# Adjacency, row and biases written into PSUM banks ahead of TensorE, in a four-layer graph kernel

## The chip, the cores and the metric

The kernel runs on one core of a Trainium2 chip. The metric is the device time of that core in microseconds. Before the change it is 4798.81 us, the median of three runs (4797.05 to 4799.08).

## The reference

Sixty-four graphs of 256 nodes with 128 features go through four layers, float32 throughout. All share one weighted adjacency matrix `adj` (256 x 256). Each layer is pre-normalised and residual: `h = relu(layernorm(x))`, `x = x + layer(h)`.

- Layer 0 is a gated recurrent graph network of five steps: a node mix `adj @ h`, two sigmoid gates, a tanh candidate, `h = (1 - z) h + z hv`.
- Layer 1 mixes `h` with Chebyshev powers of `adj`, multiplies by weights, adds `bias1` and takes the ReLU.
- Layer 2 computes `(adj @ h + h) @ weight + bias2` and divides each row by its norm.
- Layer 3 is an attention over all pairs of nodes:

```python
pre = s1[:, :, None, :] + s2[:, None, :, :] + b_lin     # 256 x 256 pairs x 256 features
h = jnp.where(pre >= 0, pre, ALPHA * pre)
e = jnp.einsum('bije,e->bij', h, a) + bias              # bias is adj
attn = jax.nn.softmax(e, axis=2)
out = jax.nn.sigmoid(jnp.einsum('bij,bjf->bif', attn, x))
```

Layer 3 is most of the work: for each graph 65,536 pairs of nodes times 256 features, a nonlinearity, and a sum over features.

## The kernel before, in words

Graphs are worked on two at a time: 32 pairs of graphs. For each pair a *front* computes layers 0 to 2 and the operands of layer 3. The first pair's two graphs have a front each (called alone). Then come the scores. A *unit* is half a pair's scores: 128 nodes of each of the two graphs against all 256 nodes, so there are 64 units, and each has one PSUM bank of 128 x 512 values that gathers its scores. A unit has 32 rows of slots with two halves of the features each, 64 half-slots. A *tile* is 128 features x 4 rows x 2 x 256 nodes (128 x 2048 values): a minimum or a ReLU of one operand against a per-partition scalar. Three engines make tiles in parallel: VectorE in one instruction (L928, one operand in PSUM, one in SBUF), ScalarE in eight (L940), GpSimd in eight (L945). For 600 slots the two halves are added by a DMA that GpSimd issues (L965). TensorE then multiplies each tile by a window of the weight vector and accumulates the result into the unit's bank (L1004).

When a unit's bank is complete, its *tail* (`tail`, L803) adds the *linear row*, a part of the score that depends only on the second node (`lin`, a half of the tile `rows`, spread to all partitions by DMA): L809. It then adds the last feature (L814), takes the maximum, the exponential, the product with the nodes' values, and writes the output.

The adjacency comes into the bank first of all: at a unit's first tile, `score` (L989) takes a bank and lets TensorE multiply the identity by `adj_n` (L998, in the helper L403), with the flag that starts an accumulation. `side_by_side` (L400) makes each 128-wide product of four 32-wide matmuls.

In the front, layer 1's products go into a bank by `project_token`, and VectorE adds `bias1` in place (L664) before it forms `x2`. Layer 2 does the same with `bias2` (L687), after which ScalarE squares it.

There are eight banks. One holds an operand of ScalarE's tiles for the whole run, one an operand of VectorE's tiles for as long as a pair needs it, at most two belong to units (`banks_of`), and the rest goes round among fronts and tails.

The order of instructions on each engine is fixed when the program is built, by a planner. It keeps a clock for each engine. `ran` (L107) adds the assumed duration of a piece of work, and returns when others may count on its result: the end, a constant for each engine, and for ScalarE a lag (`behind`) that grows by 2.4% of its work and shrinks while it has nothing to do. Fronts and tails are generators that yield the engine of their next step and the time from which it may run. The main loop takes the engine whose clock is earliest and gives it the first ready thing by rank: tails, fronts, scores or row additions, tiles. Engines run their queues in this order and wait for each other by semaphores.

Of the kernel before, what the change touches and what calls it, by code (L numbers as in the profile page):

```python
# [32 lines left out]
def kernel(  # L33
# [87 lines left out]
    def take():  # L121

        spare.sort(key=lambda b: b[1])
        return spare.pop(0)
# [280 lines left out]
    def flat(t):  # L405
        return t.rearrange("p b n -> p (b n)")

    def project(pp, w, t, start=True, stop=True):

        side_by_side(pp[:, 0:t.shape[1] * N], w, flat(t), start, stop)  # L410

    def mix_nodes(pm, h, a):

        nb = h.shape[1]
        pm = by_feature(pm, nb)
# [20 lines left out]
    def project_token(pp, pairs):  # L436

        nb = pairs[0][0].shape[1]
        pp = by_token(pp, nb)
# [45 lines left out]
    def front(p, batches):  # L485
# [165 lines left out]
        hT, t = copied("hT", b, t, bufs=4)  # L651
        yield PE, t_h, 1
# [5 lines left out]
        yield PE, t, 1  # L658
        po = take()
        project_token(po[0], [(hT, th[:, 0, :]), (c1T, th[:, 1, :]), (c2T, th[:, 2, :])])  # L660
        t = ran(PE, PRODUCTS[nb], t, po[1])
        yield DVE, t
        pt = rows_of(turned_of(po))
        nc.vector.tensor_add(pt, pt, bias1.unsqueeze(1).to_broadcast([P, nb * NC, D]))  # L664
        t = ran(DVE, ELEMENTS[nb], t)
        yield DVE, t
# [7 lines left out]
        t = yield from norm(x2, t, h)  # L674
        yield PE, t, 1
# [5 lines left out]
        yield PE, t, 1  # L681
        po = take()
        project_token(po[0], [(yT, w2)])
        t = ran(PE, PRODUCT[nb], t, po[1])
        yield DVE, t
        pt = rows_of(turned_of(po))
        nc.vector.tensor_add(pt, pt, bias2.unsqueeze(1).to_broadcast([P, nb * NC, D]))  # L687
        t = ran(DVE, ELEMENTS[nb], t)
# [114 lines left out]
    def tail(u, pe, since):  # L803

        ops = READY[u]
        x3, h3, pe, lin = ops["x3"], ops["h3"], [by_feature(pe[0])[:, k, :] for k in range(NB)], ops["lin"]
        yield DVE, max(since, ops["t_lin"])
        used = banks_of.pop(u)
        nc.vector.tensor_add(by_feature(used), by_feature(used), lin.to_broadcast([P, NB, N]) if ops["alone"] else lin)  # L809
        t = ran(DVE, ELEMENTS[2], since, ops["t_lin"])  # L810
        yield DVE, t
# [3 lines left out]
        t = ran(DVE, 0.8, t)  # L815
# [156 lines left out]

    def score_ready():

        best = None
        for tile_ in made:
            u, _ = where(tile_[1])
            since = tile_[0]
            if u not in left:
                if len(banks_of) == 2 or not spare:  # L980
                    continue
                since = max(since, min(b[1] for b in spare))
            if best is None or since < best[0]:
                best = since, tile_
        return best
# [3 lines left out]
    def score(tile_):  # L989
        since, n, k, t, e = tile_  # L990
        u, r = where(n)
        made.remove(tile_)
        if u not in left:
            left[u] = 64
            bank, free = take()
            banks_of[u] = bank
            for x, (_, c) in enumerate(across(u)):
                side_by_side(by_feature(bank)[:, x, :], ident, adj_n[:, c, :], x == 0, False)  # L998
            ran(PE, 0.87, since, free)
        left[u] -= 2 if k == 2 else 1  # L1000
        pe = banks_of[u]
        w = win if e == ACT else win_n
        for g in range(4):
            nc.tensor.matmul(pe[g * 32:(g + 1) * 32, :], w[:, 31 - r:63 - r], flat(t[:, g]),  # L1004
                             start=False, stop=(left[u] == 0), skip_group_check=True)
# [26 lines left out]
    def chain_ready(key, e):  # L1032

        engine, since, bank, gate = (*CHAINS[key][1], 0, None)[:4] if len(CHAINS[key][1]) < 4 else CHAINS[key][1]
        if engine != e or bank and not spare or gate and not gate():
            return None
# [5 lines left out]
        return max(since, min(b[1] for b in spare)) if bank else since  # L1042
# [15 lines left out]
    while scored[0] < 2 * NSLOT or CHAINS:  # L1058
# [20 lines left out]
        if ready:  # L1079
# [5 lines left out]
            elif e == PE:  # L1085
                score(what)
            elif rank == 2:
# [39 lines left out]
```

## Time and profile before

| | |
|---|---|
| median of 3 runs | 4798.81 us |
| the profiled execution, its own time | 4796.37 us |
| its span | 4794.6 us |
| TensorE matmul busy | 4744.3 us (99%) |
| VectorE busy | 4651.6 us (97%) |
| ScalarE busy | 4608.6 us (96%) |
| GpSimd busy | 4636.5 us (97%) |
| granted TensorE clock, mean | 0.999 |

The engines are PE (TensorE's matmuls), PEld (its weight loads), DVE (VectorE), ACT (ScalarE), POOL (GpSimd) and SP (SyncE). L928 means line 928 of the kernel before. A group's line has the engine, the operation, what is written from what, the shapes and the count, then the busy time, the mean of one, and the idle time in front of it with what ended it. Busy time counts what is in flight: an instruction that overlaps the one before it looks longer than the step from start to start. The ends of matmuls are modelled.

### The profile page before, as it was taken

The page shows a single profiled execution, that of the slowest core. Times are in us where ns is not written, and L with a number is a line of the kernel's source. Part 1 is how long each engine was busy: PE and PEld are TensorE (multiplying, and loading weights), DVE is VectorE, ACT ScalarE, POOL GpSimd, SP SyncE. Part 2 cuts the span into 40 slices and gives each one's busy share as a digit, 9 for nine tenths or more (in the row PEclk, how much of TensorE's full clock was granted, in tenths as well). Part 3 has the DMA queues.
Part 4 walks back from the last instruction along what each step waited for, and adds up shares of the span by engine and source line. Part 5 has one row for each costly group of instructions (what it writes and reads, how often), then busy time and mean ns, then how long its engine had stood idle before and what let it go on. Part 6 is the DMA issues. An engine that isn't in the chain of part 4 may idle for free.

```text
span 4794.6 us, 134766 instructions
## 1 busy us (share of the span) xinstructions
PE 4744.3 (99%) x52583; PEld 1758.2 (37%) x52583; DVE 4651.6 (97%) x3568; ACT 4608.6 (96%) x12063; POOL 4636.5 (97%) x9919
## 2 busy tenths in 40 slices
PE   9999999999999999999999999999999999999999
PEld 4333333433333333333333333333333333333333
DVE  6999999999999999999999999999999999999999
ACT  6999999999999999999999999999999999999999
POOL 3999999999999999999999999999999999999998
PEclk9999999999999999999999999999999999999999
DMA  1767777777676777777777777777767777777730
GB/s 39 151 142 154 150 146 150 145 145 158 141 157 143 143 155 152 151 146 145 149 152 149 147 150 146 151 155 146 148 138 158 150 151 151 148 150 143 151 66 5
DMA packets 131529, 672.82 MB, mean 140 GB/s; under 512 B 14920, under 2 KB 50120, under 8 KB 54088
## 3 DMA queue, kind: packets, MB, share of 16 engines
q0 software_dynamic: 86400, 629.18, 65.6%
q1 hardware_dynamic: 43768, 35.01, 2.5%
q8 instruction: 411, 6.73, 0.6%
q14 instruction: 230, 1.88, 0.1%
q10 hardware_dynamic: 720, 0.00, 0.0%
HBM read 26.48 MB, written 8.52 MB: 7 GB/s over the span
## 4 chain that ended last, share of the span: by engine, by line
PE 69%; DVE 10%; POOL 8%; DMA 6%; ACT 5%; issue 2%; POOLq 0%; SPq 0%; DVEq 0%; ACTq 0%
PE bank L1004 43%; PE bank L403 23%; DVE rl L928 8%; POOL rl L945 7%; DMA rl<-rl 5%; ACT rl L940 3%; PE bank L434 2%; PE bank L426 1%; POOL rl L965 1%; ACT h L478 0%; DVE bank L613 0%; DVE d L609 0%; DVE hT L617 0%; DVE rh L574 0%; POOL mv L398 0%
## 5 line engine op out<-in xcount | busy, mean ns | idle before, releaser
L940 ACT ACTIVATE rl<-bank,s1b 128x256 f32<-128x256 f32 x9976 | 3937.4, 704 | 47.5 <-DMA rl<-rl 18.7
L928 DVE TENSOR_TENSOR rl<-s1a,bank 128x2048 f32<-128x2048 f32 x1747 | 3909.3, 2276 | 41.4 <-DMA rl<-rl 19.5
L945 POOL TENSOR_SCALAR rl<-s2n,s1b 128x256 f32<-128x256 f32 x6408 | 3056.0, 799 | 19.5 <-ACT s1b L780 5.1
L1004 PE MATMUL bank<-rl,win_n 128*32 128x512 f32 x17992 | 2241.6, 593 | 20.8 <-DMA rl<-rl 14.9
L1004 PE MATMUL bank<-rl,win 128*32 128x512 f32 x9976 | 1317.3, 593 | 0.0
L945 POOL TENSOR_SCALAR rl<-s2c,s1a 128x256 f32<-128x256 f32 x2408 | 1167.1, 763 | 3.5
L1004 PEld LDWEIGHTS bank<-rl,win_n 128*32 128x32 f32 x17992 | 577.4, 110 | 1197.8 <-issue 978.2
L965 POOL DMA_DIRECT2D rl<-rl x600 | 644.9, 1090 | 3.6 <-PE bank L1004 0.9
L1004 PEld LDWEIGHTS bank<-rl,win 128*32 128x32 f32 x9976 | 324.8, 110 | 636.4 <-issue 516.5
L403 PE MATMUL bank<-mT,wts 128*32 128x512 f32 x2480 | 328.1, 592 | 0.5 <-ACT mT L526 0.5
L403 PE MATMUL bank<-adj_t,h 128*32 128x256 f32 x4960 | 296.8, 379 | 3.8 <-ACT h L628 3.8
L403 PEld LDWEIGHTS bank<-adj_t,h 128*32 128x32 f32 x4960 | 160.0, 110 | 160.8 <-issue 49.6
L478 ACT ACTIVATE h<-x,mv 128x128 f32<-128x128 f32 x376 | 163.8, 584 | 26.8 <-POOL mv L474 26.5
L403 PE MATMUL bank<-mT,w 128*32 128x512 f32 x1240 | 165.3, 593 | 0.6 <-ACT bank L570 0.5
L570 ACT ACTIVATE bank<-bank,gate_b 128x512 f32<-128x512 f32 (+1 forms) x165 | 137.6, 834 | 29.4 <-PE bank L403 16.5
L403 PE MATMUL bank<-rh,u5t 128*32 128x512 f32 x1240 | 164.9, 592 | 0.0
L403 PE MATMUL bank<-hT,wts 128*32 128x512 f32 x1240 | 163.5, 593 | 0.0
L403 PEld LDWEIGHTS bank<-mT,wts 128*32 128x32 f32 x2480 | 82.3, 110 | 185.1 <-issue 149.4
L398 POOL TENSOR_TENSOR mv<-mv,minus_half 128x4 f32<-128x4 f32 (+1 forms) x132 | 133.8, 1014 | 11.0
L593 ACT ACTIVATE bank<-bank,gate_b 128x512 f32<-128x512 f32 (+1 forms) x165 | 134.6, 816 | 10.2 <-PE bank L403 10.1
L526 ACT COPY mT<-bank 128x512 f32<-128x512 f32 x155 | 123.8, 799 | 19.6 <-PE bank L403 19.6
L606 ACT ACTIVATE bank<-bank,gate_b 128x512 f32<-128x512 f32 x155 | 128.8, 831 | 6.3 <-PE bank L403 6.3
(206 smaller groups left out, 3274.2 us busy)
## 6 DMA issues: line engine op xcount, KB each, us to landing
rl<-rl POOLq DMA_DIRECT2D x600, 1024.0 KB, 8.3
rows<-row SPq DMA_DIRECT2D x31, 512.0 KB
xin<-in_x_dram SPq DMA_DIRECT2D x64, 128.0 KB
out_dram<-o SPq DMA_DIRECT2D x64, 128.0 KB
row<-quarter SPq DMA_DIRECT2D x62, 2.0 KB
rows<-row SPq DMA_DIRECT2D x2, 256.0 KB
w_raw<-in_L_gnn_w_w_dram SPq DMA_DIRECT2D x3, 128.0 KB
rl<-in_L_gnn_Theta_dram SPq DMA_DIRECT2D x1, 320.0 KB
```

What stands on the lines that cost most here:

```text
L398: nc.gpsimd.tensor_tensor(t, t, minus_half[:, 0:t.shape[1]], op=OP.pow)
L403: nc.tensor.matmul(o[g:g + 32], w[:, g:g + 32], t, start=start, stop=stop, skip_group_check=True)
L478: nc.scalar.activation(h[:, k, :], s[:, k, :], AF.Relu, bias=mv[:, k, 0:1], scale=mv[:, k, 1:2])
L526: nc.scalar.copy(c, seen(bank))
L570: nc.scalar.activation(seen(r), seen(pr), AF.Tanh, bias=br, scale=0.5)
L593: nc.scalar.activation(seen(pr), seen(pr), AF.Tanh, bias=bz, scale=0.5)
L606: nc.scalar.activation(seen(pv), seen(pv), AF.Tanh, bias=bh_n, scale=-1.0)
L928: nc.vector.tensor_tensor(t, rows.to_broadcast(whole), ops["s2a"].unsqueeze(1).to_broadcast(whole), op=OP.min)
L940: nc.scalar.activation(t[:, g, b, :], other(ops["s2p"][0], b), AF.Relu, bias=rows[:, g, b], scale=-1.0)
L945: nc.gpsimd.tensor_scalar(t[:, part, b, :], other(ops["s2n" if k else "s2c"], b), rows[:, part, b], MOST_NEGATIVE, op0=OP.min, op1=OP.max)
L965: nc.gpsimd.dma_start(out=t.rearrange("p g b n -> p (g b n)"), in_=z.rearrange("p g b n -> p (g b n)"), accum_op=OP.add)
L1004: nc.tensor.matmul(pe[g * 32:(g + 1) * 32, :], w[:, 31 - r:63 - r], flat(t[:, g]), start=False, stop=(left[u] == 0), skip_group_check=True)
```

## The change

Three things change.

- **Adjacency and row.** For all units but the first pair's two, TensorE's product of identity and `adj_n` goes away. Instead VectorE writes `adj_n + lin` into the unit's bank before its first tile is scored (`fill_bank`, when `bank_ready` allows it). TensorE accumulates onto it from the first tile. The addition of the row in the tail goes away.
- **Biases.** For all fronts but the first pair's, ScalarE copies `bias1` or `bias2` into the bank that the products will use, and TensorE accumulates onto it. VectorE's two additions go away. The bank is taken before the last node mix instead of after it.
- **The planner.** ScalarE's lag goes away. Banks that a matmul has filled completely are kept in a set, `WRITTEN`, and only those are used for banks that another engine writes first. In the node mix and the token product only the first matmul of the whole bank carries the starting flag.

```diff
 SEEN = {PE: 0.25, DVE: 0.14, ACT: 0.18, POOL: 0.13}
-    behind = [0.0]
 
     def ran(engine, us, *after):
         start = max(clock[engine], 0.0, *after)
-        if engine == ACT:
-            behind[0] = max(0.0, behind[0] - (start - clock[ACT])) + 0.024 * us
         clock[engine] = start + us
-        return clock[engine] + SEEN[engine] + (behind[0] if engine == ACT else 0.0)
+        return clock[engine] + SEEN[engine]
...
-    def take():
-
-        spare.sort(key=lambda b: b[1])
-        return spare.pop(0)
+    WRITTEN = set()
+
+    def of_spare(bank):
+
+        return [b for b in spare if bank < 2 or id(b[0]) in WRITTEN]
+
+    def take(bank=1):
+
+        b = min(of_spare(bank), key=lambda b: (max(b[1], min(now.values())), bank < 2 and id(b[0]) in WRITTEN, b[1]))
+        spare.remove(b)
+        if bank < 2:
+            WRITTEN.discard(id(b[0]))
+        return b
+
+    def written(bank, nb):
+
+        if nb == NB:
+            WRITTEN.add(id(bank))
...
-                side_by_side(pm[:, b, :], h[:, b, c, :], a[:, c, :], c == 0, c == NC - 1)
+                side_by_side(pm[:, b, :], h[:, b, c, :], a[:, c, :], b == c == 0, c == NC - 1)
...
-                    side_by_side(pp[:, b, c, :], t[:, b, c * P:(c + 1) * P], w, k == 0, k == len(pairs) - 1)
+                    side_by_side(pp[:, b, c, :], t[:, b, c * P:(c + 1) * P], w, fresh and b == c == k == 0, k == len(pairs) - 1)
...
         hT, t = copied("hT", b, t, bufs=4)
+        if not alone:
+            yield ACT, t, 2
+            po = take(2)
+            nc.scalar.copy(rows_of(turned_of(po)), bias1.unsqueeze(1).to_broadcast([P, nb * NC, D]))
+            t_po = ran(ACT, COPY[nb], po[1])
         yield PE, t_h, 1
         b = take()
         mix_nodes(b[0], h, adj_2)
...
         yield DVE, t
-        pt = rows_of(turned_of(po))
-        nc.vector.tensor_add(pt, pt, bias1.unsqueeze(1).to_broadcast([P, nb * NC, D]))
-        t = ran(DVE, ELEMENTS[nb], t)
-        yield DVE, t
+        if alone:
+            pt = rows_of(turned_of(po))
+            nc.vector.tensor_add(pt, pt, bias1.unsqueeze(1).to_broadcast([P, nb * NC, D]))
+            t = ran(DVE, ELEMENTS[nb], t)
+            yield DVE, t
...
         yield DVE, max(since, ops["t_lin"])
-        used = banks_of.pop(u)
-        nc.vector.tensor_add(by_feature(used), by_feature(used), lin.to_broadcast([P, NB, N]) if ops["alone"] else lin)
-        t = ran(DVE, ELEMENTS[2], since, ops["t_lin"])
-        yield DVE, t
+        used = banks_of.pop(u)[0]
+        if ops["alone"]:
+            nc.vector.tensor_add(by_feature(used), by_feature(used), ops["lin"].to_broadcast([P, NB, N]))
+            since = ran(DVE, ELEMENTS[2], since, ops["t_lin"])
+            yield DVE, since
...
+    UNITS = [where(n)[0] for n in range(0, NSLOT, SLOTS // 2)]
+
+    def bank_ready():
+
+        u = next((u for u in UNITS if u not in left and u not in banks_of), None)
+        if u not in READY or READY[u]["alone"] or len(banks_of) == 2 or all(where(slot(k))[0] < u for k in range(3)):
+            return None
+        return (max(READY[u]["t_lin"], min(b[1] for b in of_spare(2))), u) if of_spare(2) else None
+
+    def fill_bank(u):
+        bank, free = take(2)
+        nc.vector.tensor_add(by_feature(bank), adj_n[:, u[1]:u[1] + 1, :].to_broadcast([P, NB, N]), READY[u]["lin"])
+        banks_of[u] = bank, ran(DVE, ELEMENTS[2], free, READY[u]["t_lin"])
...
-        if u not in left:
-            left[u] = 64
+        if u not in banks_of:
             bank, free = take()
-            banks_of[u] = bank
+            banks_of[u] = bank, free
             for x, (_, c) in enumerate(across(u)):
                 side_by_side(by_feature(bank)[:, x, :], ident, adj_n[:, c, :], x == 0, False)
             ran(PE, 0.87, since, free)
+            written(bank, NB)
+        left.setdefault(u, 64)
...
+            if e == DVE and bank_ready():
+                todo.append((bank_ready()[0], (2,), bank_ready()[1]))
```

More of the change, by code (lines that the diff above doesn't have):

```diff
@@ L410, in project @@
         side_by_side(pp[:, 0:t.shape[1] * N], w, flat(t), start, stop)
+        written(pp, t.shape[1])
     def mix_nodes(pm, h, a):
         nb = h.shape[1]
+        written(pm, nb)
         pm = by_feature(pm, nb)
@@ L434, in to_token, with project_token @@
                 nc.tensor.transpose(pt[:, b, c, :], ht[:, b, c * P:(c + 1) * P], ident)
-    def project_token(pp, pairs):
+    def project_token(pp, pairs, fresh=True):
         nb = pairs[0][0].shape[1]
+        written(pp, nb)
         pp = by_token(pp, nb)
@@ L657, in front @@
         c2T, t = copied("c2T", b, t)
[L658 to L661, printed above, removed]
-        yield DVE, t
-        pt = rows_of(turned_of(po))
-        nc.vector.tensor_add(pt, pt, bias1.unsqueeze(1).to_broadcast([P, nb * NC, D]))
-        t = ran(DVE, ELEMENTS[nb], t)
-        yield DVE, t
+        yield PE, t if alone else max(t, t_po), alone
+        if alone:
+            po = take()
+            t_po = po[1]
+        project_token(po[0], [(hT, th[:, 0, :]), (c1T, th[:, 1, :]), (c2T, th[:, 2, :])], fresh=alone)
+        t = ran(PE, PRODUCTS[nb], t, t_po)
+        yield DVE, t
+        if alone:
+            pt = rows_of(turned_of(po))
+            nc.vector.tensor_add(pt, pt, bias1.unsqueeze(1).to_broadcast([P, nb * NC, D]))
+            t = ran(DVE, ELEMENTS[nb], t)
+            yield DVE, t
         x2 = token("x2", tag="x12", bufs=3)
@@ L674, in front @@
         t = yield from norm(x2, t, h)
+        if not alone:
+            yield ACT, t, 2
+            po = take(2)
+            pt = rows_of(turned_of(po))
+            nc.scalar.copy(pt, bias2.unsqueeze(1).to_broadcast([P, nb * NC, D]))
+            t_po = ran(ACT, COPY[nb], po[1])
         yield PE, t, 1
@@ L680, in front @@
         yT, t = copied("yT", b, t)
[L681 to L684, printed above, removed]
-        yield DVE, t
-        pt = rows_of(turned_of(po))
-        nc.vector.tensor_add(pt, pt, bias2.unsqueeze(1).to_broadcast([P, nb * NC, D]))
-        t = ran(DVE, ELEMENTS[nb], t)
+        yield PE, t if alone else max(t, t_po), alone
+        if alone:
+            po = take()
+            t_po = po[1]
+        project_token(po[0], [(yT, w2)], fresh=alone)
+        t = ran(PE, PRODUCT[nb], t, t_po)
+        if alone:
+            yield DVE, t
+            pt = rows_of(turned_of(po))
+            nc.vector.tensor_add(pt, pt, bias2.unsqueeze(1).to_broadcast([P, nb * NC, D]))
+            t = ran(DVE, ELEMENTS[nb], t)
         yield ACT, t
@@ L805, in tail @@
         ops = READY[u]
-        x3, h3, pe, lin = ops["x3"], ops["h3"], [by_feature(pe[0])[:, k, :] for k in range(NB)], ops["lin"]
+        x3, h3, pe = ops["x3"], ops["h3"], [by_feature(pe[0])[:, k, :] for k in range(NB)]
         yield DVE, max(since, ops["t_lin"])
-        used = banks_of.pop(u)
-        nc.vector.tensor_add(by_feature(used), by_feature(used), lin.to_broadcast([P, NB, N]) if ops["alone"] else lin)
-        t = ran(DVE, ELEMENTS[2], since, ops["t_lin"])
-        yield DVE, t
+        used = banks_of.pop(u)[0]
[3 more added lines that the diff above has]
+            yield DVE, since
         sc = feat("sc", **SHORT)
@@ L814, in tail @@
             nc.vector.scalar_tensor_tensor(sc[:, k, :], ops["s2o"][:, b, :], ops["s1o"][:, b, c:c + 1], pe[k], op0=OP.min, op1=OP.add)
-        t = ran(DVE, 0.8, t)
+        t = ran(DVE, 0.8, since)
         spare.append([used, t])
@@ L979, in score_ready @@
             if u not in left:
-                if len(banks_of) == 2 or not spare:
+                if not READY[u]["alone"] and u not in banks_of or READY[u]["alone"] and (len(banks_of) == 2 or not spare):
                     continue
-                since = max(since, min(b[1] for b in spare))
+                since = max(since, banks_of[u][1] if u in banks_of else min(b[1] for b in spare))
             if best is None or since < best[0]:
@@ L999, in score @@
             ran(PE, 0.87, since, free)
+            written(bank, NB)
+        left.setdefault(u, 64)
         left[u] -= 2 if k == 2 else 1
-        pe = banks_of[u]
+        pe = banks_of[u][0]
         w = win if e == ACT else win_n
@@ L1034, in chain_ready @@
         engine, since, bank, gate = (*CHAINS[key][1], 0, None)[:4] if len(CHAINS[key][1]) < 4 else CHAINS[key][1]
-        if engine != e or bank and not spare or gate and not gate():
+        free = of_spare(bank)
+        if engine != e or bank and not free or gate and not gate():
             return None
@@ L1041, in chain_ready @@
                 return None
-        return max(since, min(b[1] for b in spare)) if bank else since
+        return max(since, min(b[1] for b in free)) if bank else since
     def advance(key):
@@ L1086 @@
                 score(what)
+            elif e == DVE and rank == 2:
+                fill_bank(what)
             elif rank == 2:
```

## The prediction

> **What bounds the kernel now.** I read the page's first part, then busy time by stretch, then the waits of single engines, then the costly groups, and last the timeline for the step from one instruction to the next. The first part says only that four engines are full:
>
> ```profile
> PE 4744.3 (99%) x52583; PEld 1758.2 (37%) x52583; DVE 4651.6 (97%) x3568; ACT 4608.6 (96%) x12063; POOL 4636.5 (97%) x9919
> ```
>
> Busy time by stretch separates start, middle and end (columns: the stretch, its length, busy us of PE, PEld, DVE, ACT, POOL, granted clock, DMA share, GB/s):
>
> ```profile
> 0.00:80.00 80.00, 73.49 (x993) 38.69 (x997) 40.54 (x133) 37.54 (x85) 8.82 (x29) 1.00 0.11 28
> 80.00:160.00 80.00, 77.28 (x990) 32.35 (x983) 72.75 (x68) 74.95 (x198) 68.54 (x150) 1.00 0.52 107
> 160.00:4640.00 4480.00, 4448.49 (x49258) 1635.51 (x49254) 4396.13 (x3289) 4351.94 (x11392) 4424.01 (x9440) 1.00 0.72 148
> 4750.00:4795.00 45.00, 35.40 (x349) 13.13 (x342) 32.62 (x22) 34.30 (x94) 25.09 (x56) 0.90 0.03 7
> ```
>
> GpSimd has almost nothing to do for 80 us, and then stands still for 56 of 4480 us. VectorE is idle for 84 us and ScalarE for 128 us of the same stretch. PE's 31 us is too small, because its busy time counts modelled ends. The waits of each engine between 160 and 4640 us say why; each line has the total, how many, and the longest:
>
> ```profile
> POOL rl L945 <- DMA rl<-rl: 3.7, 5, 1.3
> DVE rl L928 <- DMA rl<-rl: 19.1, 25, 1.7
> ACT h L478 <- POOL mv L474: 29.8, 39, 3.0
> ACT rl L940 <- DMA rl<-rl: 18.7, 17, 3.7
> ```
>
> GpSimd's longest wait totals 3.7 us; the rest of its idle time lies around its own small norm operations. The others' waits go back to GpSimd, directly (L474) or through the row additions that it issues (DMA). So GpSimd leads and three nearly full engines follow. The groups:
>
> ```profile
> L945 POOL TENSOR_SCALAR rl<-s2n,s1b 128x256 f32<-128x256 f32 x6408 | 3056.0, 799 | 19.5 <-ACT s1b L780 5.1 <-DMA rl<-rl 3.7 <-PE bank L1004 1.3
> L403 PE MATMUL bank<-adj_n,ident 128*32 128x256 f32 x1024 | 68.7, 380 | 0.0
> L809 DVE TENSOR_TENSOR bank<-bank,rows 128x512 f32<-128x512 f32 x64 | 44.3, 693 | 8.4 <-PE bank L1004 8.1
> L687 DVE TENSOR_TENSOR bank<-bank,bias 128x512 f32<-128x512 f32 x31 | 21.5, 693 | 2.2 <-PE bank L403 2.2
> L664 DVE TENSOR_TENSOR bank<-bank,bias 128x512 f32<-128x512 f32 x31 | 21.5, 692 | 5.4 <-PE bank L403 5.1 <-ACT rl L940 0.3
> L935 ACT COPY bank<-s2n 128x512 f32<-128x512 f32 x31 | 20.9, 675 | 0.7
> ```
>
> A mean of one includes overlap with its neighbour, so it is too long for a sum. The step is read off the timeline (start, length, engine):
>
> ```profile
> 4596.12 3.61 POOL L945 TENSOR_SCALAR rl<-s2n,s1b 128x256 f32<-128x256 f32 x8
> 4599.72 3.60 POOL L945 TENSOR_SCALAR rl<-s2c,s1a 128x256 f32<-128x256 f32 x8
> ...
> 4593.44 1.05 PE L403 MATMUL bank<-adj_n,ident 128*32 128x256 f32 x16
> 4594.30 1.04 PE L1004 MATMUL bank<-rl,win_n 128*32 128x512 f32 x8
> ...
> 2403.24 0.69 DVE L809 TENSOR_TENSOR bank<-bank,rows 128x512 f32<-128x512 f32 x1
> 2403.84 0.68 DVE L574 SCALAR_TENSOR_TENSOR rh<-bank,hT 128x512 f32<-128x512 f32 x1
> ...
> 2419.43 3.08 ACT L940 ACTIVATE rl<-bank,s1b 128x256 f32<-128x256 f32 x8
> 2422.29 0.41 ACT L745 ACTIVATE s1o<-turned,odd_one 128x4 f32<-128x4 f32 x1
> ```
>
> One L945 costs GpSimd 3.60 / 8 = 0.45 us, like clockwork; the adjacency of a unit costs PE 0.86 us; a 128x512 addition costs VectorE 0.60 us; one L940 costs ScalarE (2422.29 - 2419.43) / 8 = 0.36 us. At 0.45 us, L945's 8816 instructions are 3960 us, 84% of GpSimd's 4715 us after the start.
>
> [...] In the steady part before, no VectorE instruction has two SBUF inputs (L928, L809, L664, L704, L814 each have one operand in PSUM), and GpSimd's 0.45 us never varies[...].
>
> **The change, part by part.** Counts are those of the two built instruction orders.
>
> TensorE loses the adjacency of 62 of 64 units: 62 x 0.86 = 53 us less. PE follows, so this only opens room.
>
> VectorE loses 62 bias additions, 62 x 0.60 = 37 us, and 2 of 1747 L928 tiles, 2 x 2.2 = 4 us. In 62 tails the addition of the row leaves, and 62 fills come, which add adjacency and row into a bank: also 128x512, also two tensors[...]. Bounds for one fill: 0.5 us (a little under the 0.55 us that 512 elements take at the rate of L928, 2.2 us for 2048) and, if it must wait for one GpSimd instruction, 0.60 + 0.45 = 1.05 us. I take 0.8 us: VectorE's sum is 41 - 62 x 0.2 = 29 us less. It stays a follower.
>
> ScalarE gains 62 bias copies. The nearest row, L935, gives 0.68 us; a plain 128x512 copy steps in 0.47 us (L526 at 4572.52, next start 4572.99). That is 29 to 42 us; I take 0.5 us, 31 us. It also gains 104 L940, 104 x 0.36 = 37 us: the planner, without the lag, gives it 13 more tiles. Together 68 us on the engine with 128 us of idle time in the middle. The copies stand ahead of a node mix that takes longer than they do, so they hide; queued behind each are L940 tiles, for which PE waits if they are late.
>
> GpSimd loses 104 L945 of one form and gains 16 of the other: 88 x 0.45 = 39.5 us less. The 600 issues of row additions stay, and SyncE's transfers stay at the same number, a little reordered.
>
> Now the cost that no line shows: a fill reads adjacency and row from SBUF while GpSimd runs. [...] GpSimd loses about the 0.55 us of the fill's reading, whenever it is in L945: 62 x 0.84 x 0.55 = 29 us. Bounds: 0, if nothing contends; 62 x 0.8 = 50 us[...]. I take 29 us[...].
>
> The sum on the leader: -39.5 + 29 = -10.5 us. The span of 4794.6 us becomes 4784, the profiled execution's 4796.4 us becomes 4786, and the median, 2.4 us above that execution, 4798.8 - 10.5 = 4788 us. What is late next is GpSimd again, with PE and VectorE some 40 us behind it.
>
> **The rivals.** *No contention.* The fills cost GpSimd nothing: 4798.8 - 39.5 = 4759 us, if the others keep up. For it: PE (-53) and VectorE (-41) lose at least as much. Against it: [...] ScalarE, which would then have to wait less than now. Range 4750 to 4768.
>
> *ScalarE takes the lead: slower.* Its busy time becomes 4608.6 + 68 = 4677 us. It is idle for 58 us at start and end (42.5, 5, 10.7). At 4788 us that leaves about 51 us for waits in the middle, where it has 128 us today, part of them tails of its own instructions. If the removed lag makes other engines stand for ScalarE's results at the moment planned, its waits don't shrink: all 128 kept gives 4677 + 58 + 128 = 4863 us, half of the excess kept 4825 us. It decides from about 60 us of remaining waits.
>
> *VectorE starves: slower.* GpSimd stands in runs of 8 to 16 instructions, 3.6 to 7.2 us. [...] it waits half of one, some 3.5 us: 62 x 3.5 = 217 us. VectorE has 84 + 41 = 125 us of room, so it decides from 2 us for one fill, and gives 4798.8 + 217 - 125 = about 4890 us at the full price, or 4830 us at 2.5 us with PE held up behind it.
>
> *The change doesn't do what it says:* the counts show that it does; only the two first units keep the old form.
>
> **How the numbers follow.** About 0.2%, 9.6 us, is what a measurement of this kernel can tell from no change: 4789.2 to 4808.4 counts as the same. My forecast (a contended fill) has a chance of 0.45 and its own range, 0.4 to 0.8 us of loss in a fill with others' small delays, is 4776 to 4808; 4788 lies just at the edge, so I split it 0.25 faster and 0.20 same. No contention: 0.30, nearly all faster. ScalarE in the lead: 0.14, of which 0.02 is hardly visible. Starved VectorE: 0.11. Faster 0.54, same 0.22, slower 0.24. For 8 in 10 the range must take in the case without contention at its lower end and half of the slower cases: 4750 to 4830 us.
>
> **What would show it.** Right: in the timeline after, GpSimd's L945 runs, 0.45 us each elsewhere, are stretched by 0.4 to 0.8 us where a fill stands, and the fill's mean lies above 0.69 us; GpSimd still waits for nobody. No contention: the fill at 0.69 us and unbroken runs. ScalarE in the lead: ScalarE's idle time in the middle below 50 us and more waits of PE for L940. Starvation: fills of 2 us or more. Wrong altogether would be a new wait at the bias copies or at the banks: PE waiting for them, or VectorE's fill waiting for a bank.

## The result and the profile after

| | before | after |
|---|---|---|
| median, 15 runs each | 4797.69 us (4794.80 to 4799.47) | 4817.18 us (4791.60 to 4831.17) |
| ratio, 95% interval | | 1.0034 [1.0024, 1.0044] |
| the profiled execution, its span | 4796.37, 4794.6 us | 4808.59, 4806.8 us |
| mean of one fill (L1016) | | 1.516 us |
| granted TensorE clock, mean | 0.999 | 0.997 |

The kernel is slower by 0.34%, where the forecast was faster by 0.2%. The runs of after also spread over 40 us, those of before over 5 us. The medians, not the profiled execution, carry the ratio: that execution lies 9 us below the median. A second measurement on another chip gave 4814.98 us against 4803.38 us, ratio 1.0027 [1.0017, 1.0037]. Because the kernel before itself took 4797, 4815 and 4803 us on the three chips of the experiments, kernels are compared by ratios below, each to the kernel before on the same chip.

Lines have moved: L928, L940, L945, L965, L1004, L434 and L617 of before are L960, L972, L977, L997, L1051, L447 and L631 of after. The fill is L1016, the bias copies are L669 and L701. The first part of the page of after:

```profile
PE 4721.8 (98%) x51591; PEld 1741.3 (36%) x51591; DVE 4661.8 (97%) x3504; ACT 4670.0 (97%) x12229; POOL 4622.3 (96%) x9831
```

ScalarE is 61 us busier (the prediction's step says 68), GpSimd 14 us less. VectorE has 64 instructions fewer and is nevertheless 10 us busier. Busy time by stretch, with the columns of before:

```profile
160.00:4640.00 4480.00, 4410.31 (x48204) 1603.33 (x48200) 4394.61 (x3222) 4405.35 (x11536) 4395.57 (x9323) 1.00 0.72 148
```

In the middle every engine now stands still for some 70 us or more: VectorE 85, ScalarE 75, GpSimd 84 (before: 56), PE 70. So nobody leads through the whole stretch any more. Where do these pauses come from? The waits of all engines between 160 and 4640 us (total, how many, longest):

```profile
PE bank L447 <- DVE hT L631: 30.4, 10, 7.2
ACT h L642 <- PE bank L447: 27.9, 10, 7.2
```

PE's wait for `hT` was 5.8 us in 15 waits before (L434 for L617), none over 0.7 us. Now one of them alone is 7.2 us. The waits of GpSimd over the whole execution:

```profile
POOL rl L997 <- DVE rl L960: 17.4, 7, 3.9
POOL rn L408 <- DVE rn L726: 9.5, 3, 6.3
POOL rl L977 <- PE bank L1051: 7.1, 7, 2.3
```

The first line is new: GpSimd stands for a tile of VectorE, which before was 0.3 us (L965 for L928). The third was 1.3 us. The second has another cause, for it is as long (10.9 us) in the fill in two steps below, whose fills are never late. The groups say why VectorE is late:

```profile
L1016 DVE TENSOR_TENSOR bank<-adj_n,rows 128x512 f32<-128x512 f32 x62 | 94.0, 1516 | 0.0
L669 ACT COPY bank<-bias 128x512 f32<-128x512 f32 x31 | 27.2, 876 | 0.0
L701 ACT COPY bank<-bias 128x512 f32<-128x512 f32 x31 | 22.0, 710 | 0.0
```

A fill averages 1.5 us, more than twice the 0.69 us of an addition with one operand in PSUM. The view of that one line has the shortest, the median and the longest in ns:

```profile
L1016 DVE TENSOR_TENSOR bank<-adj_n,rows x62: 680/810/10116, 231.8 to 4675.1; 128x512 f32<-128x512 f32 x62
```

The mean is no typical fill. By start and end of each of the 62 in the trace, 51 take 0.68 to 1.11 us, as forecast, and cost VectorE 5.3 us more than 0.69 us each. The other 11 take 1.6 to 10.1 us and cost it 45.8 us more. An ordinary fill in the timeline (start, length):

```profile
1933.87 0.68 DVE L588 SCALAR_TENSOR_TENSOR rh<-bank,hT 128x512 f32<-128x512 f32 x1
1934.39 1.76 POOL L977 TENSOR_SCALAR rl<-s2n,s1b 128x256 f32<-128x256 f32 x2
1934.46 0.69 DVE L1016 TENSOR_TENSOR bank<-adj_n,rows 128x512 f32<-128x512 f32 x1
1935.06 4.48 DVE L960 TENSOR_TENSOR rl<-s1a,bank 128x2048 f32<-128x2048 f32 x2
```

VectorE is served at once. GpSimd pays: its step beside the fill (from one start to the next) is 0.99 us instead of 0.45. And one of the eleven, with GpSimd and PE beside it:

```profile
2151.88 10.03 POOL L977 TENSOR_SCALAR rl<-s2n,s1b 128x256 f32<-128x256 f32 x20
...
2153.60 0.68 DVE L623 TENSOR_TENSOR d<-bank,hT 128x512 f32<-128x512 f32 x1
2154.20 7.41 DVE L1016 TENSOR_TENSOR bank<-adj_n,rows 128x512 f32<-128x512 f32 x1
...
2155.09 2.76 PE L1051 MATMUL bank<-rl,win_n 128*32 128x512 f32 x24
2161.52 0.69 DVE L627 SCALAR_TENSOR_TENSOR bank<-bank,d 128x512 f32<-128x512 f32 x1
2162.12 2.27 DVE L960 TENSOR_TENSOR rl<-s1a,bank 128x2048 f32<-128x2048 f32 x1
2164.31 0.68 DVE L631 SCALAR_TENSOR_TENSOR hT<-bank,hT 128x512 f32<-128x512 f32 x1
...
2164.93 0.88 POOL L997 DMA_DIRECT2D rl<-rl  x1 [3.02 <-DVE rl L960]
2165.05 1.11 PE L447 MATMUL bank<-ident,hT 128*128 128x128 f32 x4 [7.21 <-DVE hT L631]
```

Read it from the top. The fill starts at 2154.20, and GpSimd goes on making its tiles at 0.45 us each, without giving way. The last of them starts at 2160.39, and the instruction after it (L997) must itself wait. Only there does the fill end, at 2161.6. Of the eleven, four end like this one, at a pause of GpSimd; the other seven are served in the middle of its run, after it has gone past them with 3 to 22 instructions, and then one step of it is 0.88 to 0.99 us. Behind the fill on VectorE stand L627, a tile and `hT`. PE ran out of work at 2157.8 and waits for `hT` until 2165.05. GpSimd loses 3.02 us as well: L997, the issue of a row addition, waits for the tile at 2162.12, which stood behind the fill. It is the same in all four: L997 starts 0.54 us after the end of a tile that VectorE makes behind the fill. GpSimd keeps VectorE out and then waits for VectorE. The stall has an aftermath; the same stretches show it by their granted clock (first of the last three columns):

```profile
2157.00:2165.00 8.00, 0.84 (x8) 0.00 (x0) 8.00 (x5) 3.25 (x9) 4.98 (x12) 0.88 0.00 0
2165.00:2169.00 4.00, 3.95 (x20) 1.51 (x24) 4.00 (x2) 2.80 (x8) 4.00 (x9) 0.50 0.76 154
2169.00:2172.00 3.00, 3.00 (x44) 1.28 (x40) 3.00 (x3) 2.88 (x8) 2.57 (x6) 0.84 0.74 150
2172.00:2176.00 4.00, 4.00 (x44) 1.09 (x39) 4.00 (x3) 4.00 (x12) 2.90 (x7) 1.00 0.40 80
```

PE stood for 7.2 us, its clock was 0.50 in the next 4 us, 0.84 in the 3 us after that, and then 1.00. The other four pauses of PE over 2.5 us between 160 and 4640 us (4.4 to 5.5 us long) have 0.50 behind them too: after the one of 5.5 us, which ends at 242.10, for the next 4 us.

### The profile page after: what moved, and what is told of

Read it like the earlier page. It is cut to its first block, busy times and chain, and to the rows that moved or that the text cites. A ratio compares the mean times of both kernels' runs of the same rounds, so it can differ in the third digit from the quotient of the medians.

```text
span 4806.8 us, 132615 instructions
## 1 busy us (share of the span) xinstructions
PE 4721.8 (98%) x51591; PEld 1741.3 (36%) x51591; DVE 4661.8 (97%) x3504; ACT 4670.0 (97%) x12229; POOL 4622.3 (96%) x9831
## 4 chain that ended last, share of the span: by engine, by line
PE 56%; POOL 15%; ACT 12%; DVE 9%; DMA 5%; issue 3%; POOLq 0%; DVEq 0%; ACTq 0%
PE bank L1051 35%; PE bank L414 18%; POOL rl L977 13%; ACT rl L972 9%; DVE rl L960 7%; DMA rl<-rl 5%; PE bank L447 2%; POOL rl L997 2%; ACT h L492 1%; PE bank L439 1%; POOL mv L409 1%; DVE bank L1016 0%; ACT bank L620 0%; ACT bank L607 0%; DVE bank L627 0%
## 5 line engine op out<-in xcount | busy, mean ns | idle before, releaser
L972 ACT ACTIVATE rl<-bank,s1b 128x256 f32<-128x256 f32 x10080 | 4032.6, 762 | 16.7 <-DMA rl<-rl 13.2
L960 DVE TENSOR_TENSOR rl<-s1a,bank 128x2048 f32<-128x2048 f32 x1745 | 3898.6, 2276 | 14.2 <-PE bank L1051 7.0
L977 POOL TENSOR_SCALAR rl<-s2n,s1b 128x256 f32<-128x256 f32 x6304 | 3035.2, 820 | 13.5 <-PE bank L1051 3.7
L1051 PE MATMUL bank<-rl,win_n 128*32 128x512 f32 x17888 | 2242.9, 595 | 23.9 <-DMA rl<-rl 15.4
L1051 PE MATMUL bank<-rl,win 128*32 128x512 f32 x10080 | 1359.6, 595 | 0.8 <-issue 0.5
L977 POOL TENSOR_SCALAR rl<-s2c,s1a 128x256 f32<-128x256 f32 x2424 | 1170.1, 739 | 6.8 <-PE bank L1051 3.4
L1051 PEld LDWEIGHTS bank<-rl,win_n 128*32 128x32 f32 x17888 | 587.3, 110 | 1181.5 <-issue 969.8
L997 POOL DMA_DIRECT2D rl<-rl x600 | 635.3, 1079 | 27.3 <-DVE rl L960 17.4
L1051 PEld LDWEIGHTS bank<-rl,win 128*32 128x32 f32 x10080 | 337.8, 110 | 671.9 <-issue 514.8
L584 ACT ACTIVATE bank<-bank,gate_b 128x512 f32<-128x512 f32 (+1 forms) x165 | 145.0, 879 | 17.4 <-PE bank L414 13.4
L607 ACT ACTIVATE bank<-bank,gate_b 128x512 f32<-128x512 f32 (+1 forms) x165 | 140.1, 849 | 7.6 <-PE bank L414 7.3
L540 ACT COPY mT<-bank 128x512 f32<-128x512 f32 x155 | 135.4, 873 | 11.9 <-PE bank L414 11.8
L642 ACT COPY h<-bank 128x512 f32<-128x512 f32 x124 | 111.2, 897 | 29.1 <-PE bank L447 29.0
```

Source lines behind the costliest of these rows:

```text
L540: nc.scalar.copy(c, seen(bank))
L584: nc.scalar.activation(seen(r), seen(pr), AF.Tanh, bias=br, scale=0.5)
L607: nc.scalar.activation(seen(pr), seen(pr), AF.Tanh, bias=bz, scale=0.5)
L642: nc.scalar.copy(h, turned_of(b))
L960: nc.vector.tensor_tensor(t, rows.to_broadcast(whole), ops["s2a"].unsqueeze(1).to_broadcast(whole), op=OP.min)
L972: nc.scalar.activation(t[:, g, b, :], other(ops["s2p"][0], b), AF.Relu, bias=rows[:, g, b], scale=-1.0)
```

## Experiments

**Theories.** A: the two SBUF inputs of the fill are the cause, where they meet GpSimd's work (its step beside the fill at 1934.46 was 0.99 us). Without them the forecast's case without contention, 4759 us, should appear. The rivals: B, the planner without the lag makes ScalarE or others wait; C, the banks are now scarce or are taken too early; D, moving the biases to ScalarE costs more than the 31 us of its copies.

**The fill in two steps.** The same sum in the same bank, but each instruction has at most one SBUF input. VectorE has one more instruction for each fill:

```diff
-        nc.vector.tensor_add(by_feature(bank), adj_n[:, u[1]:u[1] + 1, :].to_broadcast([P, NB, N]), READY[u]["lin"])
+        nc.vector.tensor_copy(by_feature(bank), adj_n[:, u[1]:u[1] + 1, :].to_broadcast([P, NB, N]))
+        nc.vector.tensor_add(by_feature(bank), by_feature(bank), READY[u]["lin"])
```

> The changed kernel with its 62 fills in two instructions, a copy of the adjacency and an addition of the row to the bank, so that no VectorE instruction has two SBUF inputs; the order of all else is the same. It gives VectorE 62 x 0.60 = 37 us of work more. Theory S: no fill is longer than 0.8 us, GpSimd's step stays 0.45 us, the runs lie within 10 us of each other, and the time is that of GpSimd's smaller work, 4798 - 40 = 4758, plus up to 25 for a VectorE as full as before: 4760 to 4785 us. Rival L (the planner without the lag makes engines wait for ScalarE): as the changed kernel or 37 us slower, 4815 to 4850 us, with the same spread of runs. Rival B (banks taken ahead): 4810 or more, since banks are taken as early as in the changed kernel.

Measured: 4757.26 us (4755.60 to 4757.57), ratio 0.9916 [0.9903, 0.9930]. The groups of this kernel:

```profile
L1017 DVE TENSOR_TENSOR bank<-bank,rows 128x512 f32<-128x512 f32 x62 | 43.4, 699 | 2.2
L1016 DVE COPY bank<-adj_n 128x512 f32<-128x512 f32 x62 | 42.4, 684 | 0.0
```

Neither step is ever over 0.70 us, and the runs agree within 2 us again. Planner, banks, biases and ScalarE's work are those of after. By the traces, so is the order of instructions on VectorE, ScalarE and GpSimd, with two instructions in the place of each fill. This is the cleanest comparison: nothing is taken away but the second SBUF input. So B, C and D are not what makes after slow: two instructions for each fill are faster than one by 1.2%, some 57 us. That the two SBUF inputs are the cause is shown here; whether GpSimd has to do with it is the question of the next two runs.

**The two inputs by themselves.** Not the reference's computation: the output is zeros. GpSimd runs 1800 steps like L945; beside it VectorE makes tiles and 40 additions with one operand in PSUM, then 40 with both in SBUF:

```diff
+    for k in range(STREAM):
+        nc.gpsimd.tensor_scalar(made[:, k % 8, :], s2n, col[:, 0:1], -3.0e38, op0=OP.min, op1=OP.max)
+    for _ in range(GROUPS):
+        tiles()
+        nc.vector.tensor_add(bank, held, rows)                  # L51, held in PSUM
+    for _ in range(GROUPS):
+        tiles()
+        nc.vector.tensor_add(bank, adj_n[:, 0:1, :].to_broadcast([P, 2, N]), rows)   # L54
```

> This kernel leaves out the whole computation (its output is zeros) and measures the disputed cost alone: GpSimd runs 1800 minima of 128x256 from SBUF without a gap, VectorE runs four tiles of 128x2048 with one operand in PSUM and then one 128x512 addition, 80 times; in the first 40 the addition reads PSUM and SBUF, in the last 40 it reads SBUF twice. Nothing waits for anything by semaphore. Theory S ([...] VectorE is now and then kept out for a whole run of GpSimd): the first 40 additions take 0.69 us and GpSimd keeps its step of 0.45 us; of the last 40 most take 0.7 to 1.1 us with one GpSimd step of 0.9 to 1.0 us beside each, and some take 4 us or more while GpSimd keeps 0.45 us. Rival B (the long fills are waits for banks): all 80 take 0.69 us and GpSimd's step never changes.

Measured: 835.74 us in one execution. The two groups of additions, and GpSimd's run beside four of the second kind in the timeline:

```profile
L54 DVE TENSOR_TENSOR bank<-adj_n,rows 128x512 f32<-128x512 f32 x40 | 27.7, 693 | 0.0
L51 DVE TENSOR_TENSOR bank<-held,rows 128x512 f32<-128x512 f32 x40 | 27.7, 692 | 0.0
```

```profile
400.43 12.68 POOL L42 TENSOR_SCALAR made<-s2n,col 128x256 f32<-128x256 f32 x22
400.44 0.69 DVE L54 TENSOR_TENSOR bank<-adj_n,rows 128x512 f32<-128x512 f32 x1
...
403.24 0.69 DVE L54 TENSOR_TENSOR bank<-adj_n,rows 128x512 f32<-128x512 f32 x1
```

VectorE sees no difference at all. GpSimd does: beside each of the 40 fills one step is 1.01 us instead of 0.45, while the 40 additions with a PSUM operand leave its step at 0.4495 us. Here are the prediction's 29 us (62 x 0.84 x 0.56 = 29 us), and no starvation. But in the order of the built program only one tile stands between two fills, so they came every 2.80 us, always at one place in GpSimd's step (0.00 to 0.01 us after its start). This run could not say what a fill at another place meets.

**The two inputs at all places.** The same, with a copy of a varying length ahead of each of 75 fills, and a pause of GpSimd after every 24 steps. The output is zeros again.

```diff
+        n = 16 + 10 * (k * 7 % FILLS)
+        nc.vector.tensor_copy(short[:, 0:n], flat[:, 0:n])
         nc.vector.tensor_add(bank, adj_n[:, 0:1, :].to_broadcast([P, 2, N]), rows)
```

> This kernel leaves out the whole computation (its output is zeros). As in the first measurement alone GpSimd runs minima of 128x256 without a gap, with a tiny write after each 24, and VectorE adds two SBUF operands of 128x512 into a bank, 75 times; but a copy of a length that changes from time to time stands ahead of each addition, so that it arrives at all phases of GpSimd's 0.45 us step. Theory S in its first form[...]: most additions take 0.69 to 1.1 us and cost GpSimd 0.5 to 0.56 us; those that arrive 0.08 to 0.16 us and 0.36 to 0.46 us after a start of GpSimd's (as the long ones in the changed kernel do) can take 1.5 us or more, up to the 11 us to the next tiny write. Rival P (the long ones need something of the full kernel, TensorE, ScalarE or the DMA): none takes longer than 1.2 us here.

Measured: 807.22 us. The longest of the 75 in the timeline:

```profile
66.64 6.39 POOL L61 TENSOR_SCALAR made<-s2n,col 128x256 f32<-128x256 f32 x13
68.19 0.68 DVE L69 COPY short<-long_one 128x506 f32<-128x506 f32 x1
68.79 3.99 DVE L70 TENSOR_TENSOR bank<-adj_n,rows 128x512 f32<-128x512 f32 x1
72.69 2.27 DVE L67 TENSOR_TENSOR work<-col,held 128x2048 f32<-128x2048 f32 x1
72.97 0.10 POOL L63 MEMSET mark<- 128x4 f32 x1
```

Starvation (an engine is kept out again and again) exists without the rest of the kernel: this fill ends only where GpSimd's run ends. It is rarer, though. Of 75 fills, three take over 1.15 us (1.50, 1.93 and 3.99 us), all of which began 0.36 to 0.43 us after a start of GpSimd; but 12 of the 15 that began in the same stretch took at most 1.05 us. In the kernel it is 11 of 62, up to 10.1 us, and they began 0.08 to 0.49 us after a start, which is nearly anywhere in a step of 0.45 us. The place in the step alone does not decide.

**No fill.** The banks are never filled ahead; TensorE multiplies the adjacency and the tail adds the row, as before. Biases and planner stay changed. In `bank_ready`:

```diff
-        if u not in READY or READY[u]["alone"] or len(banks_of) == 2 or all(where(slot(k))[0] < u for k in range(3)):
+        if True or u not in READY or READY[u]["alone"] or len(banks_of) == 2 or all(where(slot(k))[0] < u for k in range(3)):
             return None
```

> The changed kernel with the adjacency by TensorE at the first tile and the row in the tail, as before; biases by ScalarE and no lag as after. By its order GpSimd has 32 tile instructions less than before (14 us), VectorE 17 us less, ScalarE 17 us more, TensorE as before. Theory S: 4778 to 4795 us with runs within 10 us of each other. Rival L: 4808 us or more. Rival B (the bias banks taken ahead): 4808 us or more.

Measured: 4803.37 us (21 runs, 4799.51 to 4805.91), ratio 1.0011 [1.0005, 1.0018]: a miss, above the expected 4778 to 4795 us. The waits of this kernel between 160 and 4640 us:

```profile
ACT rl L971 <- PE bank L1050: 30.2, 35, 1.9
DVE rl L959 <- PE bank L1050: 26.2, 49, 2.6
```

Before, the same two waits were 9.3 and 13.6 us. GpSimd has 32 instructions of L945's kind fewer than before, and its busy time is 13 us less, but its own waits are 104.7 us instead of 88.3, and ScalarE and VectorE now wait for buffers that PE frees late. I had not counted PE's room as needed. This run speaks for it: with the adjacency's 53 us on PE, less work for GpSimd brought nothing. It does not isolate it, for its plan also gives GpSimd 56 tile instructions (25 us) more than the two steps, which are part of the distance from 0.9916 to 1.0011.

**The lag alone.** The kernel before, with only the lag taken out of `ran`:

```diff
-        return clock[engine] + SEEN[engine] + (behind[0] if engine == ACT else 0.0)
+        return clock[engine] + SEEN[engine]
```

> The kernel before with the growing lag of ScalarE taken out of the planner and nothing else. By its order GpSimd has 16 tile instructions less than before (7 us), VectorE nine tiles less (20 us), ScalarE 88 instructions more (32 us). Theory S: 4785 to 4800 us, no slower than before. Rival L: 4808 us or more, with more waits for ScalarE's results.

Measured: 4792.30 us (13 runs, 4790.64 to 4794.80), ratio 0.9990 [0.9982, 0.9998]. GpSimd makes 16 instructions fewer, 16 x 0.45 = 7 us, and 5 us are seen. Rival B falls here too.

**The fill alone.** The kernel before with nothing changed but the fill: the lag and VectorE's bias additions are back (the conditions on `alone` in the front become constants, and `behind` returns in `ran`).

```diff
-        if not alone:
+        if False:
             yield ACT, t, 2
...
-        if alone:
+        if True:
             pt = rows_of(turned_of(po))
```

> Only the fill of the change: adjacency and row by VectorE ahead of TensorE, biases by VectorE afterwards as before, and the planner with its lag. GpSimd has 16 tile instructions less than before (7 us). Theory S: 4798 - 7 plus 40 to 70 us for the two SBUF inputs: 4830 to 4860 us, with a spread of runs of 20 us or more. Rival L (the lag or the loaded ScalarE): 4785 to 4800 us with little spread.

Measured: 4882.97 us (4882.02 to 4887.22), with 4814.72 us (4796.11 to 4814.96) for the kernel before on that chip: ratio 1.0141 [1.0124, 1.0158], just above what I expected. The four runs lie within 5 us, where I had expected a spread of 20 or more. The group of the fills:

```profile
L1019 DVE TENSOR_TENSOR bank<-adj_n,rows 128x512 f32<-128x512 f32 x62 | 92.4, 1491 | 0.8 <-DMA rows<-row 0.8
```

The fills are as long as in after (12 of 62 over 1.5 us), so their length does not need the bias copies or the missing lag. They cost at least 1.4% here, against the kernel before, where after loses 1.2% against the two steps. VectorE also has the 37 us of bias additions here. I take that as the reason, but no run isolates it, and the plan is another one.

**The fill twice.** The same instruction, issued two times:

```diff
         nc.vector.tensor_add(by_feature(bank), adj_n[:, u[1]:u[1] + 1, :].to_broadcast([P, NB, N]), READY[u]["lin"])
+        nc.vector.tensor_add(by_feature(bank), adj_n[:, u[1]:u[1] + 1, :].to_broadcast([P, NB, N]), READY[u]["lin"])
```

> The changed kernel with the addition of each fill carried out twice, the second writing the same values again: 62 more VectorE instructions with two SBUF inputs. Against the version in two steps (4757 us), which has as many VectorE instructions, everything on top is the cost of two SBUF inputs. Theory S: twice the 51 us between the profiled runs of the changed kernel and of the two-step version, 4850 to 4880 us, with at least 15 instructions of the fill longer than 1.5 us. Rival L or B: 4817 us or up to 37 us more for the added work.

Measured: 4852.38 us (4846.48 to 4855.80), ratio 1.0077 [1.0062, 1.0092]. Against the case without contention (0.9916) that is 1.6%, where the single fill has 1.2%: not doubled. (In microseconds it lies within the expected 4850 to 4880, but the kernel before takes 17 us more on this chip.) The groups:

```profile
L1016 DVE TENSOR_TENSOR bank<-adj_n,rows 128x512 f32<-128x512 f32 x62 | 100.0, 1612 | 0.0
L1017 DVE TENSOR_TENSOR bank<-adj_n,rows 128x512 f32<-128x512 f32 x62 | 58.3, 940 | 2.1
```

The first of each pair behaves as in after: 15 of 62 over 1.5 us, 52.7 us of excess. Of the second ones only 2 do. They follow directly on a fill that was served: 56 of the 62 begin 0.43 to 0.80 us after a start of GpSimd, nearly all of them inside its long step. That may be why they starve so rarely; no run isolates it. Both cost GpSimd about alike: its busy time is 4597.9 us with the two steps, 4622.3 us in after and 4649.3 us here, so the first fills add 24.4 us and the second ones 27.0 us. My expectation of double took the starvation for a price of each instruction; 15 of the 62 first ones paid it and 2 of the 62 second ones.

**ScalarE writes the adjacency.** It copies the adjacency into the bank, the row is added in the tail again, and GpSimd's norm is planned at 2.2 and 1.9 us instead of 1.69 and 1.35:

```diff
-        nc.vector.tensor_add(by_feature(bank), adj_n[:, u[1]:u[1] + 1, :].to_broadcast([P, NB, N]), READY[u]["lin"])
-        banks_of[u] = bank, ran(DVE, ELEMENTS[2], free, READY[u]["t_lin"])
+        nc.scalar.copy(by_feature(bank), adj_n[:, u[1]:u[1] + 1, :].to_broadcast([P, NB, N]))
+        banks_of[u] = bank, ran(ACT, COPY[2], free)
```

> A version that uses what the runs showed: ScalarE copies the adjacency into the bank ahead of TensorE, VectorE adds the row in the tail as before, so that no VectorE instruction has two SBUF inputs; the planner counts GpSimd's norm at 2.2 and 1.9 us in place of 1.69 and 1.35[...]. By its order GpSimd has 112 tile instructions less than the two-step version (50 us), VectorE 6 us less, ScalarE 30 us more. If GpSimd still led, 4757 - 50 = 4707 us; with ScalarE and VectorE as full as they are, 4725 to 4755 us. If ScalarE becomes the one that all wait for: 4760 to 4785 us.

Measured: 4774.35 us (4773.74 to 4776.06), ratio 0.9917 [0.9902, 0.9932]. Busy time between 160 and 4640 us in this kernel:

```profile
160.00:4640.00 4480.00, 4458.06 (x48540) 1648.53 (x48532) 4409.39 (x3255) 4468.69 (x11679) 4386.23 (x9302) 1.00 0.72 148
```

By the ratio, a way around the two inputs by another engine gains as much as the two steps. In microseconds it is 17 more than theirs. Of the seven runs of the kernel before on this chip six took about 4814 us and one took 4796, so how well ratios carry from chip to chip is not shown. ScalarE now leads (4469 of 4480 us), which the prediction's rival *ScalarE takes the lead* had feared of the change itself.

**The adjacency held in PSUM.** One bank keeps both halves of the adjacency for the whole run, written by the first fill. The fill remains one instruction, with one operand in PSUM and one in SBUF:

```diff
-        nc.vector.tensor_add(by_feature(bank), adj_n[:, u[1]:u[1] + 1, :].to_broadcast([P, NB, N]), READY[u]["lin"])
+        nc.vector.tensor_add(by_feature(bank), by_feature(HELD[0])[:, u[1]:u[1] + 1, :].to_broadcast([P, NB, N]), READY[u]["lin"])
```

> The changed kernel with the adjacency copied once into a PSUM bank of its own, and each fill reading it there: the fill stays one addition, at the same place in the same order, but has one operand in PSUM and one in SBUF. One bank less goes round. Theory S: as the version in two steps, since GpSimd leads: about 0.9916 of the time before, 4757 us, possibly some us less as VectorE has 37 us less to do; fills of 0.69 us; GpSimd's step 0.45 us. Rival B (banks): slower than the changed kernel, as there is one bank fewer. Rival L: as the changed kernel, 1.0034.

Measured: 4762.95 us (4761.66 to 4763.78) against 4803.38 us for the kernel before on that chip, ratio 0.9915 [0.9902, 0.9928]. The view of that one line (shortest, median, longest):

```profile
L1022 DVE TENSOR_TENSOR bank<-bank,rows x62: 686/691/699, 232.7 to 4626.9; 128x512 f32<-128x512 f32 x62
```

Each fill is still one instruction and differs only in the memory of one operand. I had expected the order of after around it. It is another one: with a bank fewer the planner decides otherwise, and 1050 of VectorE's 3507 places hold another instruction. All fills take 0.69 us, the runs agree within 2 us, and 1.2% are gone. With the two steps, which keep the order, this shows the two SBUF inputs as the cause. By what mechanism they hold up GpSimd is not shown; what the runs show is that GpSimd's step grows to 1.01 us beside such a fill and stays at 0.4495 us beside one with an operand in PSUM (both in the run of the two inputs by themselves). Rival C falls too: the kernel has a bank fewer and loses nothing. It equals the two steps, although VectorE is 38 us less busy (4611.2 against 4648.9 us), so VectorE is not what bounds either.

**Held in PSUM, and the norm planned at its length.** GpSimd's two pieces of norm work are planned at 1.69 and 1.35 us. In the trace of after they take 2.23 and 1.65 us of GpSimd's time (medians, from start to start). Here they are planned at 2.2 and 1.9 us on top of the last kernel:

```diff
-        t = ran(POOL, 1.69, t)
+        t = ran(POOL, 2.2, t)
...
-        t = ran(POOL, 1.35, t) + 0.1
+        t = ran(POOL, 1.9, t) + 0.1
```

> The same with GpSimd's norm counted at 2.2 and 1.9 us in the planner. By its order GpSimd has 136 tile instructions less than the version before it in this list (61 us), ScalarE 64 more (23 us), VectorE nine tiles more (20 us). If GpSimd leads and all others follow: 4757 - 61 = 4696 us. ScalarE was idle for 27 us of 4480 in the two-step version, so I expect ScalarE to take the lead: 0.986 to 0.992 of the time before, 4730 to 4757 us.

Measured: 4773.97 us (4773.30 to 4775.99), ratio 0.9939 [0.9926, 0.9952]: worse than without, and above the expected 0.986 to 0.992. Busy time in the middle of this kernel:

```profile
160.00:4640.00 4480.00, 4455.76 (x48530) 1648.71 (x48526) 4397.98 (x3252) 4469.96 (x11683) 4363.12 (x9279) 1.00 0.72 148
```

GpSimd was relieved (4363 us), and the work went to ScalarE, which is full with 4470 us. No plan tried here gains by taking more work from GpSimd.

**After, once more.** The same kernel as after, for comparison on the chip of the last two.

> The changed kernel once more, beside the two versions: 1.0024 to 1.0044 of the time before by the earlier comparison; again a spread of runs of 20 to 40 us and again about 10 of 62 fills longer than 1.5 us, but not the same ones, since it is chance which fill meets GpSimd at the wrong moment.

Measured: 4814.98 us (4808.80 to 4830.51), ratio 1.0027 [1.0017, 1.0037]. Again 11 of 62 fills are over 1.5 us, the longest 10.1 us. Six of them, the longest among them, are the same fills as in the first profile, five are others. I had expected chance. Since half of them recur, which fills starve is neither all chance nor all fixed by the order. The runs spread over 22 us here. Starved fills alone do not make such a spread: the kernel with the fill alone has 12 of them and its four runs lie within 5 us.

## Why the prediction was wrong

GpSimd was the leader, so its account shows each step. Busy time is from the page, waits are the sum of its lines in the profile (all us):

| GpSimd in the profiled execution | busy | waits | span |
|---|---|---|---|
| before | 4636.5 | 88.3 | 4794.6 |
| after | 4622.3 | 116.9 | 4806.8 |
| fill in two steps | 4597.9 | 87.1 | 4755.5 |
| adjacency held in PSUM | 4602.4 | 87.8 | 4761.0 |
| after less before | -14.2 | +28.6 | +12.2 |
| after less two steps | +24.4 | +29.8 | +51.3 |
| after less held in PSUM | +19.9 | +29.1 | +45.8 |

What is neither busy nor a wait, mostly before its first work, is 68 to 71 us in all four. The kernel with the adjacency in PSUM ran on another chip; against the second profile of after, from that chip, the last row is +23.4, +24.4 and +46.0 us.

- **GpSimd leads and loses 88 instructions, -39.5 us: right.** Without contention the time falls by 39.9 us in the two steps (4797.17 to 4757.26) and by 40.4 us with the adjacency in PSUM; in the two steps GpSimd's busy time falls by 38.6 us and its waits stay what they were. The others kept up, as the rival *no contention* (4759 us) assumed. That GpSimd still leads there is not shown: ScalarE stands for only 27 of the 4480 us in the middle of that kernel, GpSimd for 54.
- **The contended fill costs GpSimd 29 us: right in kind, too large in size.** It was an estimate (0.55 us, what 512 elements take at the rate of L928, for 84% of 62 fills); that a fill costs GpSimd anything, nothing in the profile of before showed. GpSimd's busy time in the last two rows of the table says 24.4 and 19.9 us. The place of the price was right: beside a served fill there is one step of 0.88 to 1.01 us for 0.45. By the starts in the traces, 48 of GpSimd's steps from one tile instruction straight to the next are over 0.5 us in after, 7 before (of 7198, so "never varies" is nearly right) and 6 with the two steps.
- **"If it must wait for one GpSimd instruction, 1.05 us": this step failed.** It set the upper bound of a fill, and with it "It stays a follower" and "GpSimd still waits for nobody". In 51 of 62 cases it holds (at most 1.11 us); in the other 11 GpSimd passes the waiting fill with up to 22 instructions, and the fill takes up to 10.1 us. The prediction allowed VectorE 62 x 0.2 = 12 us for all of it; the trace has 5.3 + 45.8 = 51 us. The step assumed that VectorE's turn comes at the end of the GpSimd instruction in flight. The 51 fit that, and the 11 do not: there 3 to 22 of GpSimd's next instructions went first. (The 0.60 us is the step from start to start, 2403.24 to 2403.84 in before; the length of that one instruction, as the fills are measured here, is 0.69 us.)
- **The rival *VectorE starves* (chance 0.11) was right in kind and wrong in price.** It took half a run for every fill, 3.5 us x 62, subtracted VectorE's whole idle time, and said that 2 us for one fill decides. The mean stayed at 1.5 us, and it was decided all the same. Idle time is no reserve that pays for a delay of 7 us at one place: PE had work for about 3.6 us at 2154.20, then stood 7.2 us and ran on at half clock. What came back to GpSimd were the 29 us of waits in the table, which the sum -39.5 + 29 did not contain. Most of them are at L997, which waits for tiles behind late fills: 17.4 us for VectorE's tile and 6.2 us that the profile gives no cause for, where the two steps have 1.5 us for both. In the profiled execution the sum on the leader was thus -38.6 + 24.4 + 28.6 = +14.4 us (the span grew by 12.2) and not -39.5 + 29 = -10.5.
- **ScalarE and biases: nearly right.** ScalarE's busy time rose by 61 us instead of 68; one copy costs it 0.51 us from start to start (0.5 taken). In after it stands for 75 us of the middle and does not lead. It is the fullest engine in the two steps, and clearly so when it is given the fills as well.
- **TensorE's -53 us "only opens room": the room seems to be needed.** With the adjacency back on PE, GpSimd has 14 us less than before and the ratio is 1.0011; the plan differs too, so no run isolates it.

The median stayed in the range of 4750 to 4830 us. The forecast's side was wrong since the starved fill was priced as a case where nearly all fills starve, or none.

Open: why fills starve more often and longer in the kernel (11 of 62) than by themselves (3 of 75). The length of GpSimd's runs and what the other engines read at the same time differ in several ways, and no run separates them. How the 51.3 us between the profiled executions of after and of the two steps, or the 57 us between the ratios, divide between the half clock and the waits themselves was not measured either. Why the runs of after spread is open too.

## What to carry to other kernels

Before an instruction of VectorE is made to read two operands from SBUF, look at whether GpSimd runs without gaps at that place. If it does, keep one operand in PSUM or split the instruction: two instructions (0.68 and 0.70 us on average) were 1.2% faster here than the one of 1.52 us, and one with an operand in PSUM (0.69 us) was as well. Price a rare wait by its longest case and by what stands behind it at that place, not by its mean against an engine's idle time.

## What was unexpected of the hardware

- A VectorE instruction with two SBUF inputs of 128x512 values waited up to 10.1 us while 22 GpSimd instructions went by at the undisturbed 0.45 us; 51 of the 62 fills took 0.68 to 1.11 us. All 62 together added 20 to 24 us to GpSimd's busy time.
- Which fill starves changed in part between executions of one program: five of the eleven were others in a second profile, six the same. The runs of after spread over 40 us, those of the same order with each fill in two steps over 2 us.
- After PE's stall of 7.2 us the granted clock was 0.50 in the next 4 us and 0.84 in the 3 us after that; behind its four other pauses of 4.4 to 5.5 us it was 0.50 as well.
